# Two groups of stores move to ScalarE's DMA queue in a four-layer graph network

## The chip, the cores and the metric

The kernel runs on one core of a Trainium2 chip. The metric is device time in microseconds (us) from the start of the program to its end, as the median of several runs. Five engines work side by side, each through its own list of instructions in order: TensorE (PE in the profile), VectorE (DVE), ScalarE (ACT), GpSimd (POOL) and SyncE (SP). SP, ACT and POOL can also issue DMA transfers, each on a queue of its own.

## The reference

A graph of 2708 nodes with 512 features goes through four layers, each of the form `x = layernorm(x + layer(x, adj))`, all in fp32. Layer 0 is a graph attention autoencoder with four heads of 128 features, and the change lies in it. Cut to what matters:

```python
Xw = einsum('hnd,hde->hne', Xh, W)
f1 = einsum('hnd,hd->hn', Xw, V[:, 0, :, 0])
f2 = einsum('hnd,hd->hn', Xw, V[:, 1, :, 0])
sig = sigmoid(f1[:, :, None] + f2[:, None, :])
att = masked_softmax(adj * sig, adj != 0)      # both patterns are adj
Xa = einsum('hij,hjd->hid', att, Xw)           # first attention pass
# batchnorm, mlp block -> emb
Y = einsum('hij,hjd->hid', att, Yh)            # second pass, same att
# times W, elu, mlp block; then layers 1, 2 and 3
```

Layer 1 multiplies by the normalised adjacency matrix, layer 2 is attention over a masked score matrix, layer 3 is full attention with the adjacency as a bias.

## The kernel before, in words

The attention matrix of layer 0 is never whole. It is formed in blocks: a block has 128 of the nodes j on the partitions (22 blocks, the last with 20 rows) and one half of the nodes i along the free axis (1354 columns). Two heads, a "pair", are done together, so a block's tile `t` has 2 x 1354 columns. The loops of `attention_pass` run over the halves `hf`, then the pairs `p`, then the 22 blocks in the order of `ORDER`, in which the short block stands in the middle.

A block is formed in `form`: the adjacency block `a` is loaded by SP (L379); when the pair is the first one of the first pass (`prepare`), VectorE marks the zeros of `a` with large negative numbers (L395, L396) and POOL stores the result to `adj_d` in DRAM (L400), from where later passes load it. ScalarE computes a tanh for each head from the broadcast row `f1b` and the column `f2h` (L407), VectorE combines it with `a` (L415), and ScalarE takes the exp in place (L416). Then TensorE multiplies by the values (L503, twelve matmuls a block) and, in the first pass, sums with a column of ones (L540). The pool of `t` has four buffers and that of `a` four in the first pass.

The exponentials of the blocks in `KEPT` are stored to DRAM as `kept_...` in the first pass (L485) and loaded in the second (L488) in place of being formed again. Of the first pair, five places of 22 are kept in each half (4, 8, 11, 14, 18), so ten stores in all, one of them in each half of the short block. Of the second pair it is eight in each half. A full store is 1354 KB.

Before the passes, `project` loads the inputs on SP's queue: the transposed features in six chunks, the weights, the first two adjacency blocks and the parameters. `f1_rows` makes the rows of f1 for a chunk (L263, copied to `stage` by VectorE in L270). Those of the first half are stored to the DRAM tensor `f1_d` (L275), and two loads on SP (L277, the variable `spread`) broadcast them to all partitions as `f1b`, one for each head of the first pair. `values_of` makes the values `xw` and the columns `f2h`; ScalarE or VectorE copies them out of PSUM (L294, L298). The last blocks' values, and the rows of f1 of the second half, are made in `rest`, whose instructions on VectorE are put behind the first block's L415.

The order on each engine is set by a scheduler that works from the program's order and estimated times, bound here and there by `tc.issue_after`, which puts an instruction behind another one on the same engine. Waits between engines and for buffers are made from the tiles' use.

Of the kernel before, what the change touches and what calls it, by code (L numbers as in the profile page):

```python
# [29 lines left out]
def gnn_stack_kernel(  # L30
# [25 lines left out]
    nc = tc.nc  # L56
    N, F = x.shape
    H = w0.shape[1]
# [119 lines left out]
    with ExitStack() as l0:  # L178
# [8 lines left out]
        f1_d = dram.tile([H, N], F32, name="f1_d")  # L187
# [31 lines left out]
        def project(att, psum):  # L219
# [39 lines left out]
            def f1_rows(ci, dst):  # L259
                c0, w = CHUNKS[ci]  # L260
                pf = psum.tile([P, BANK], F32, tag=f"psm{ci % 2}", name="pf")
                for h in range(H):
                    nc.tensor.matmul(  # L263
                        pf[32 * h : 32 * h + 32, :w],
                        wv1[:, h, :],
                        xT_sb[:, h, c0 : c0 + w],
                        start=True,
                        stop=True,
                    )
                nc.vector.tensor_copy(dst[:, :w], pf[:, :w])  # L270

            h0, w = HSPAN[0]
            for ci, (q0, _) in enumerate(HCH[0]):
                f1_rows(ci, stage[:, q0:])
            nc.sync.dma_start(f1_d[:, h0 : h0 + w], stage[0 : 32 * H : 32, :w])  # L275
            for k in range(HP):
                spread = nc.sync.dma_start(  # L277
                    f1b[k][:, :w], f1_d[k, h0 : h0 + w].partition_broadcast(P)
# [63 lines left out]
        def attention_pass(values, first, att, psum, finish, f1b=None, blocks=(), spread=None, rest=None, taken={}):  # L342
# [5 lines left out]
            def count(hf, jt, att, a=None):  # L348

                h0, w = HSPAN[hf]  # L350
                j0, n = BLOCKS[jt]
                if a is None:
                    a = att.tile([P, HW], F32, tag="a", name="a", bufs=3)
                    nc.sync.dma_start(a[:n, :w], adj_d[j0 : j0 + n, h0 : h0 + w])
                z = att.tile([P, HW], U8, tag="z", name="z", bufs=1)
                nc.vector.tensor_scalar(
                    z[:n, :w],
                    a[:n, :w],
                    -0.5 * BIG,
                    None,  # L360
                    ALU.is_lt,
                    ALU.add,
                    accum_out=zeros[:n, jt, hf : hf + 1],
                )
# [62 lines left out]
            def sum_tiles():  # L427
                return [
                    psum.tile([P, BANK], F32, tag=f"psm{k}", name="psm", bufs=1) for k in range(HP)
                ]  # L430
# [5 lines left out]
            for hf, (h0, w) in enumerate(HSPAN):  # L436
                for p in range(H // HP):
                    prepare = first and p == 0
# [25 lines left out]
                    for place, jt in enumerate(ORDER):  # L464
                        n = BLOCKS[jt][1]
# [5 lines left out]
                        tv = t[:n, :, :w]  # L471
                        kept = kept_d.get((hf, p, jt))
                        if kept is None or first:
                            rows = n if n == P else HR
                            with ExitStack() as order:

                                for ins in taken.values() if place == 2 else ():
                                    order.enter_context(tc.issue_after(ins.ins))
                                step = form(hf, p, jt, att, prepare, f1b, t[:rows, :, :w])
                            if rest is not None:  # L480
                                rest(step)
                                rest = None
                                sums = sum_tiles()
                            if kept is not None:
                                nc.gpsimd.dma_start(kept[:n, :, :w], tv)  # L485
                        else:
                            for r in range(0, P if n == P else HB * Q, P if n == P else Q):
                                nc.sync.dma_start(t[r : r + n, :, :w], kept[:n, :, :w])  # L488
                            if p == 0 and jt in KEPT[1]:
                                count(hf, jt, att)  # L490
# [118 lines left out]
        with (  # L609
            tc.tile_pool(name="att_a", bufs=2) as att,  # L610
            tc.tile_pool(name="ps_a", bufs=1, space=PSUM) as psum,
        ):
            f1b, blocks, spread, rest = project(att, psum)
            mlp_w = []
            taken = {}
            ft = feat_tile("ft")

            def keep(hf, p, po, sums):
# [49 lines left out]
                for k in range(HP):  # L668
# [4 lines left out]
                    for r, (q0, qw) in enumerate(SCH[hf]):  # L673
# [12 lines left out]
                        nc.vector.bn_stats(stats[:, h, SQ * hf + r, :], dst)  # L686

            attention_pass(xw, True, att, psum, keep, f1b, blocks, spread, rest, taken)
            scale1, mean1 = batch_scale(stats, G_ENC, "bn1")
            shift1 = batch_shift(scale1, mean1, B_ENC, "bn1")  # L690
# [31 lines left out]
        with (  # L722
# [58 lines left out]
            for ci, (c0, w) in enumerate(CHUNKS):  # L781
# [24 lines left out]
                while turned < NT and sum(BLOCKS[turned]) <= c0 + w:  # L806
                    j0, n = BLOCKS[turned]
# [54 lines left out]
            def decode(hf, p, po, rb):  # L862
# [168 lines left out]
                )  # L1031

            attention_pass(emb, False, att, psum, decode)
        dsum = small.tile([P, NT], F32, tag="dsum", name="dsum")
        nc.vector.tensor_reduce(dsum, zeros, AX.X, ALU.add)
# [8 lines left out]
    with (  # L1044
# [13 lines left out]
        with tc.tile_pool(name="l1a", bufs=1) as pre:  # L1058
# [4 lines left out]
            for ci, (c0, w) in enumerate(PIECES):  # L1063
# [10 lines left out]
                while turned < NT and sum(BLOCKS[turned]) <= c0 + w:  # L1074
                    it = turned
                    i0, n = BLOCKS[it]
# [30 lines left out]
        for g in range(0, NT, G):  # L1107
            group = range(g, min(g + G, NT))
            c0 = g * P
            w = min(N, c0 + G * P) - c0  # L1110
# [9 lines left out]
            for jt, (j0, m) in enumerate(BLOCKS):  # L1120
                if later and jt % 4 == 3:
                    y, n = later.pop(0)
# [12 lines left out]
                for it in group:  # L1135
                    n = BLOCKS[it][1]
# [9 lines left out]
            for it in group:  # L1146
                n = BLOCKS[it][1]
# [51 lines left out]
    def softmax_layer(  # L1199
# [245 lines left out]
        def end(st):  # L1445
# [19 lines left out]
            for b, it in enumerate(GROUPS[gi]):  # L1465
# [46 lines left out]
                def project(b=b, it=it, n=n):  # L1512
# [9 lines left out]
                    finish(it, ps[:n], rs[:n, b : b + 1])()  # L1522

                later.append(project)

        states = {}
# [34 lines left out]
    with (  # L1561
# [3 lines left out]
        for gi, group in enumerate(GROUPS):  # L1565
            for y, n in last_rows if gi == 1 else ():
                layer_norm(y, y, n)
            c0, w = GSPAN[gi]
            xt = work.tile([P, C, GW], F32, tag="xt", name="xt_g")
            for b, it in enumerate(group):  # L1570
                n = BLOCKS[it][1]
# [8 lines left out]
            for b, it in enumerate(group):  # L1580
                n = BLOCKS[it][1]
# [260 lines left out]
```

## Time and profile before

| | us |
|---|---|
| median of 3 runs | 3232.25 |
| lowest and highest | 3231.26 and 3234.68 |
| the profiled execution | 3233.64 |
| its span, first to last instruction | 3231.8 |

| engine | busy us | share of the span |
|---|---|---|
| PE, matmul | 3196.0 | 99% |
| DVE | 1929.0 | 60% |
| ACT | 1318.2 | 41% |
| POOL | 136.1 | 4% |

The page gives the busy time of each engine, a chain of work that ended last, and groups of instructions by line. A timeline lists instructions in order: start, length, engine, line, operation, output and inputs; in square brackets stands the idle time of the engine before the instruction and what ended it. In a chain of waits each row has a start, a length and what took it. `SPq`, `ACTq` and `POOLq` stand for an engine's sequencer, which also issues DMAs. `f_d` is the profile's name for `f1_d`, and `f_rows` for `stage`. A table of windows gives busy times, the granted TensorE clock, the mean busy share of the 16 DMA engines and what they moved, by stretch.

### The profile page before, as it was taken

What the parts mean: (1) busy time and instruction counts of PE and PEld (TensorE: products, weight loads), DVE (VectorE), ACT (ScalarE), POOL (GpSimd) and SP (SyncE); (2) the same over time, 40 slices, a digit from 0 to 9 for tenths busy, and PEclk for the clock granted to TensorE, in tenths of its full rate; (3) what the DMA queues carried; (4) which work ended last, traced back from release to release, by engine and by line L of the source; (5) the groups of instructions that cost most, each with busy time, mean ns of one, the idle gap of its engine ahead of it and who ended that gap; (6) DMA issues with size and microseconds to landing.
All of it is one profiled execution on the core that took longest, in us unless ns stands there. A gap on an engine that the chain in (4) does not pass through costs nothing.

```text
span 3231.8 us, 30335 instructions
## 1 busy us (share of the span) xinstructions
PE 3196.0 (99%) x10874; PEld 1714.4 (53%) x10874; DVE 1929.0 (60%) x3160; ACT 1318.2 (41%) x1498; POOL 136.1 (4%) x220
## 2 busy tenths in 40 slices
PE   8999999999999999999999999999999999999999
PEld 5444444444444446875555555554555555555554
DVE  7888987876686685444154677776344342542533
ACT  6898896477767451001142434442011020120211
POOL 1100100000000000000010000000000000000000
PEclk9999999999999999999999999999999999999999
DMA  8867875156546314540054444553211111111100
GB/s 284 313 218 257 292 243 198 60 178 224 198 165 210 142 57 121 144 110 1 0 155 117 128 132 139 148 161 94 75 43 32 44 35 38 43 30 46 34 24 20
DMA packets 175701, 400.35 MB, mean 124 GB/s; under 512 B 21274, under 2 KB 116454, under 8 KB 169214
## 3 DMA queue, kind: packets, MB, share of 16 engines
q1 hardware_dynamic: 158622, 315.64, 32.1%
q0 software_dynamic: 16496, 80.70, 6.5%
q8 instruction: 85, 1.39, 0.2%
q10 hardware_dynamic: 432, 2.08, 0.2%
q14 instruction: 66, 0.54, 0.1%
HBM read 315.46 MB, written 81.30 MB: 123 GB/s over the span
## 4 chain that ended last, share of the span: by engine, by line
PE 85%; issue 8%; DVE 3%; ACT 2%; DMA 1%; POOL 1%; SPq 0%; POOLq 0%; DVEq 0%; ACTq 0%
PE po L1407 24%; PE ps_s L1286 18%; PE po L503 16%; PE ps_nb L1139 7%; PE ps_wide L1188 5%; PE ps_hid L128 2%; PE ps_sup L1584 2%; PE ps_o L1515 2%; PE ps_dec L914 2%; PE ps_mlp L789 1%; PE psm L540 1%; PE ps_s L1278 1%; ACT t L416 1%; PE tp L1178 1%; DVE t L415 1%
## 5 line engine op out<-in xcount | busy, mean ns | idle before, releaser
L415 DVE SCALAR_TENSOR_TENSOR t<-t,a 128x2708 f32<-128x2708 f32 (+1 forms) x150 | 444.3, 2976 | 150.2 <-ACT t L407 145.0
L407 ACT ACTIVATE t<-f1b,f2h 128x1354 f32<-128x1354 f32 (+1 forms) x300 | 411.2, 1412 | 50.0 <-PE po L503 31.7
L503 PE MATMUL po<-t,xw 128*128 128x452 f32 (+3 forms) x1056 | 407.6, 549 | 4.7 <-ACT t L416 4.7
L416 ACT ACTIVATE t<-t 128x2708 f32<-128x2708 f32 (+1 forms) x150 | 368.0, 2455 | 99.2 <-DVE t L415 99.1
L1286 PE MATMUL ps_s<-sup,hT 128*128 128x384 f32 (+1 forms) x1176 | 407.5, 490 | 0.0
L1407 PE MATMUL po<-sup,e 128*128 128x512 f32 x882 | 407.0, 595 | 0.0
L1407 PE MATMUL po<-e,xs 128*128 128x384 f32 (+1 forms) x1176 | 406.1, 489 | 0.0
L503 PE MATMUL po<-t,emb 128*128 128x452 f32 (+3 forms) x1056 | 395.5, 543 | 3.8 <-ACT t L416 3.8
L1718 DVE SCALAR_TENSOR_TENSOR e<-a_cols,ps_s 128x384 f32<-128x384 f32 (+1 forms) x154 | 85.6, 556 | 450.5 <-PE ps_s L1286 427.7
L1286 PEld LDWEIGHTS ps_s<-sup,hT 128*128 128x128 f32 x1176 | 221.8, 190 | 164.2 <-issue 14.2
L1407 PEld LDWEIGHTS po<-e,xs 128*128 128x128 f32 x1176 | 222.2, 190 | 160.2 <-issue 5.8
L503 PEld LDWEIGHTS po<-t,xw 128*128 128x128 f32 (+1 forms) x1056 | 188.7, 189 | 212.7 <-issue 196.1
L503 PEld LDWEIGHTS po<-t,emb 128*128 128x128 f32 (+1 forms) x1056 | 192.9, 189 | 199.3 <-issue 191.2
L1407 PEld LDWEIGHTS po<-sup,e 128*128 128x128 f32 x882 | 160.4, 190 | 159.3 <-issue 137.1
L1286 PE MATMUL ps_s<-hT 128*128 128x384 f32 (+5 forms) x672 | 211.0, 461 | 0.9 <-ACT sup L1591 0.7
L1385 ACT ACTIVATE e<-e 128x384 f32<-128x384 f32 (+1 forms) x308 | 151.6, 522 | 116.4 <-DVE e L1384 113.5
L1139 PE MATMUL ps_nb<-hid_hi,at 128*128 128x512 f32 x484 | 185.4, 390 | 0.4 <-DVE at L1131 0.4
L1633 ACT ACTIVATE a_cols<-a_cols,neg_big 128x384 f32<-128x384 f32 (+1 forms) x154 | 94.6, 616 | 223.5 <-DMA a_cols<-in_adjT_dram 195.7
L1139 PE MATMUL ps_nb<-hid_lo,at 128*128 128x512 f32 x462 | 179.9, 389 | 0.0
L1384 DVE TENSOR_TENSOR e<-e,nmax 128x384 f32<-128x384 f32 (+1 forms) x308 | 163.1, 552 | 23.3 <-ACT nmax L1377 23.3
L108 ACT ACTIVATE ln_rstd<-ln_rstd 128x1 f32<-128x1 f32 (+1 forms) x88 | 17.3, 202 | 389.1 <-DVE ln_rstd L107 388.3
L1286 PEld LDWEIGHTS ps_s<-hT 128*128 128x128 f32 x672 | 123.2, 190 | 89.3 <-issue 20.8
(253 smaller groups left out, 3327.1 us busy)
## 6 DMA issues: line engine op xcount, KB each, us to landing
a<-adj_d SPq DMA_DIRECT2D x108, 677.0 KB
a_cols<-in_adjT_dram SPq DMA_DIRECT2D x378, 192.0 KB
kept<-t POOLq DMA_DIRECT2D x22, 1354.0 KB, 6.5
t<-kept SPq DMA_DIRECT2D x22, 1354.0 KB
a<-in_adjT_dram SPq DMA_DIRECT2D x42, 677.0 KB
adj_d<-a POOLq DMA_DIRECT2D x42, 677.0 KB, 5.8
raw<-in_adjT_dram SPq DMA_DIRECT2D x105, 256.0 KB
a_cols<-in_adjT_dram SPq DMA_DIRECT2D x63, 202.0 KB
```

Of the source, the lines that this page charges most:

```text
L407: tanh = nc.scalar.activation(tv[:, k, :], f1b[k][:n, :w], AF.Tanh, bias=f2h[:n, jt, h : h + 1], scale=0.5,)
L415: step = nc.vector.scalar_tensor_tensor(tv, tv, GUARD, ab, ALU.add, ALU.mult)
L416: exp = nc.scalar.activation(tv, tv, AF.Exp, scale=0.5)
L503: nc.tensor.matmul(po[HB * k + q][:, :qw], values[r : r + n, jt, h * P : (h + 1) * P], t[r : r + n, k, q0 : q0 + qw], start=(place == 0), ...
L1139: nc.tensor.matmul(pos[it][:n], at, half[:, jt, :], start=(jt == 0 and k == 0), stop=(jt == NT - 1),)
L1188: nc.tensor.matmul(ps[:, :width], w(c, o), xt(c), start=(c == 0), stop=(c == C - 1),)
L1286: nc.tensor.matmul(ps[:, b * P : w], keys[:, c, j0 : j0 + P], st["q"][:, c, b * P :], start=(c == 0), stop=(c == C - 1),)
L1384: nc.vector.tensor_tensor(e, e, st["nmax"][:, :w], ALU.add)
L1385: nc.scalar.activation(e, e, AF.Exp)
L1407: nc.tensor.matmul(out, lhsT, rhs, start=(k == 0), stop=(k == NT - 1))
L1633: nc.scalar.activation(a, a, AF.Identity, bias=neg_big[: a.shape[0]], scale=1.0e30)
L1718: nc.vector.scalar_tensor_tensor(e, a, 2.0, ps, ALU.mult, ALU.add)
```

## The change

The store of f1's rows of the first half (L275) is issued from ScalarE and not from SyncE. The ten stores of the first pair's kept exponentials (L485 with `prepare` true) are issued from ScalarE and not from GpSimd; the sixteen of the second pair stay on GpSimd. Nothing else is edited: the same bytes go to the same places, and the loads of `f1b` stay on SP.

```diff
             h0, w = HSPAN[0]
             for ci, (q0, _) in enumerate(HCH[0]):
                 f1_rows(ci, stage[:, q0:])
-            nc.sync.dma_start(f1_d[:, h0 : h0 + w], stage[0 : 32 * H : 32, :w])
+
+            nc.scalar.dma_start(f1_d[:, h0 : h0 + w], stage[0 : 32 * H : 32, :w])
             for k in range(HP):
                 spread = nc.sync.dma_start(
                     f1b[k][:, :w], f1_d[k, h0 : h0 + w].partition_broadcast(P)
...
                             if kept is not None:
-                                nc.gpsimd.dma_start(kept[:n, :, :w], tv)
+
+                                queue = nc.scalar if prepare else nc.gpsimd
+                                queue.dma_start(kept[:n, :, :w], tv)
                         else:
```

## The prediction

> **What bounds the kernel now.** I read the page first: TensorE (PE) is busy in 3196.0 of 3231.8 us, so an edit moves the end only where it moves PE's work. Then I asked for PE's idle stretches in the first 560 us, where the moved stores lie (they are issued between 18.67 and 395.95 us). PE has a start in which it runs ahead of its data, and one hole that names a store of the kept exponentials. The chain of waits over the first 45 us shows the start:
>
> ```profile
> 17.99 0.02 issue
> 18.02 0.64 DVE f_rows L270
> 18.65 0.02 issue
> 18.67 5.93 DMA f_d<-f_rows
> 24.59 0.02 issue
> 24.61 0.34 SPq L277
> 24.95 0.06 issue
> 25.01 7.73 DMA f1b<-f_d
> 32.74 0.03 issue
> 32.77 1.43 ACT t L407
> 34.20 0.02 issue
> 34.23 2.98 DVE t L415
> ```
>
> Columns are start, length, what. The store of f1's first rows is only 21.2 KB, yet it takes 5.93 us. Until it has landed SP may not issue the two broadcast loads of f1b. Those take until 32.74, then come the tanh and the first scalar_tensor_tensor (L415). The `rest` work on VectorE is queued behind that L415, and PE's first attention matmul (L503) starts at 43.38.
>
> Why 5.93 us: the table of windows for 15 to 24 us has a DMA share of 1.00 at 377 GB/s. The packet records show SP's queue without a hole until about 24, and the store's own 5416 byte packets at 23.7 to 24.1, the last of the queue. The store waits behind inputs that SP queued earlier.
>
> The second place, timelines of PE, ACT and POOL around 315 to 329 us, in this order of lines:
>
> ```profile
> 315.24 0.53 POOL L400 DMA_DIRECT2D adj_d<-a  x1 [8.28 <-DVE a L396]
> 315.76 0.53 POOL L485 DMA_DIRECT2D kept<-t  x1
> ...
> 325.06 1.43 ACT L407 ACTIVATE t<-f1b,f2h 128x1354 f32<-128x1354 f32 x1 [3.00 <-DMA kept<-t]
> ...
> 328.88 4.82 PE L503 MATMUL po<-t,xw 128*128 128x452 f32 x12 [1.89 <-ACT t L416]
> ```
>
> The exp of that block ended at 314.34 (311.88 + 2.46). POOL first waited for VectorE's adjacency block and issued that store, then the kept one 1.42 us after its exp. The kept store landed 9.20 us later. A tanh that needs the buffer waited 3.00 us, and PE 1.89 us. Other PE holes of the first pass (0.93 at 236.40, 0.96 at 363.05, 0.93 at 486.44) name an exp behind the 20-row block, not a store.
>
> [...] two queues do alternate from 34 to 36.5 us, but POOL's store issued at 29.46 moved its first packet at 33.96, after 1539 KB of SP's loads. [...] from 38 to 43 us, after 2.94 us without a matmul, the granted clock is 0.50.
>
> **Part 1: f1's rows on ACT's queue (L275).** Removed from SP: one issue of 0.64 us, and SP's wait for VectorE's copy (3.3 us), which held nothing else, as the next SP items wait for this store anyway. Added to ACT: one issue. The nearest row is ACT's own f1b load (L453, three issues of 326 to 344 ns); the dearest is SP's 0.64. In that stretch ACT does the xw copies, 0.58 us each with 0.31 us of waiting for PE between them, so three copies absorb it; without that cover it is 0.64 us. If the issue stands one copy too early in ACT's order it waits for the rows (18.65), about 2 us after the copy that begins at 16.64. Queued behind it are ten more copies; PE waits for them, as pxw has three PSUM buffers. The copies end at 28.34 and the first tanh can't begin before that, so I take 0 and keep 1 us as the upper end.
>
> Landing: issue at 18.7, first packet 1.9 us later (ACT's f1b load of 151.92 began to move at 153.85)[...], 0.5 us to the release: about 22. Bounds: [...] 24.6 if the store still waits for all of the earlier inputs. Then SP issues the f1b loads (0.84 us for both)[...], and they follow the inputs without a gap at about 24.2, and ahead of the adj_d store issued at 23.89. 1354 KB at 365 KB per us (the 377 GB/s above) are 3.7 us: landed by about 28.5, against 32.74. If they share with that store (677 KB more), by 29.8.
>
> What is late next: ACT ends its copies at 28.34, two tanh of 1.42 end at 31.2. VectorE's row decides:
>
> ```profile
> 31.53 0.69 DVE L294 COPY xw<-pxw 128x512 f32<-128x512 f32 x1 [0.98 <-PE pxw L285]
> 32.14 0.15 DVE L298 TENSOR_SCALAR f2h<-pxw 128x4 f32<-128x4 f32 x1
> 34.23 2.98 DVE L415 SCALAR_TENSOR_TENSOR t<-t,a 128x2708 f32<-128x2708 f32 x1 [1.94 <-ACT t L407]
> ```
>
> If the order on VectorE stays, L415 begins behind that copy at 32.25 and not at 34.23: 2.0 us, all of its 1.94 us wait. With L415 ahead of the copy it would begin at 31.2: 3.0 us. After it VectorE and PE go hand in hand to 43.38, so PE starts its attention earlier by the same. From 44 to 170 PE is busy in 126.00 of 126.00 us, so the shift is kept. PE's idle stretch of 2.94 us shrinks by it too; if the half clock goes with it, the 5 us at 0.50 save up to 1 us more (2.5 of PE's own time, but VectorE sets most of that stretch). I take **-2.0**, bounds 0 and -4.0.
>
> **Part 2: ten kept stores on ACT's queue (L485).** Removed from POOL: ten issues of 0.53 us; POOL is idle 96% of the time, and its adj_d stores no longer have a kept store between them. Added to ACT: ten issues of 0.33, each behind the exp it stores. Where the trace doesn't show it is the wait: the issue has to wait until the exp's writes are done, so the next tanh, now overlapping the exp's end by about 0.1 us, can't be under way:[...] 0.55 us when the store stands directly behind its exp, 0 when it stands behind the next tanh. Queued behind it are the next tanh pair, then L415 on VectorE, then exp, then PE.
>
> What covers it: PE needs 6.03 us a block in these two stages, ACT 4.98 (2 x 1.41 + 2.45, less overlaps), and ACT waits for PE to free a buffer of t: 0.94 us a block at 68.02, 74.03, 80.07, 104.13 and 110.15, and after 341.14 too. In other blocks it waits for L415, 0.4 us each from 376 to 404. All ten stores have 3 or more blocks between them, each with 1.05 us to spare. So 10 x 0.55 = 5.5 us of ACT is hidden but for the stretch around 314 us where PE has no lead: **+0.3**. Bounds 0 and +5.5 by these prices. Below nothing is possible too, and is the next point.
>
> The hole at 328.88: on ACT the store is issued at about 314.8, 1 us earlier[...]. From 315.5, a load of 677 KB, the kept 1354 and the adj_d 677 are in flight: 2708 KB at 365 are 7.4 us, all landed by 323, the kept one not last, say 322. The tanh then starts at 322 and not 325.06, and its exp ends at 325.8, before PE is ready at 326.99. The 1.89 us hole closes: **-1.9**, bounds 0 and -1.9. PE is busy before and after, so it is kept; next late is the 0.96 at 363.05, which stays.
>
> **Sum.** -2.0 + 0.3 - 1.9 = -3.6 us. The profiled execution took 3233.64 (span 3231.8 and 1.8 around it): 3230.0. It is 1.4 above the median of the three runs, 3232.25, from which the forecast is 3228.65. A measurement of this kernel can tell about 0.2% from no change, 6.5 us.
>
> **The rivals.** (a) As summed: 3228.65. Chance 0.40.
> (b) The small store still waits for inputs[...], as POOL's store of 29.46 did. Part 1 is then worth nothing: -1.9 + 0.3, 3230.65. For it: that 1539 KB row. Against: 34 to 36.5. The move is made, and does not do what it is for. Chance 0.24.
> (c) All ends are good: L415 first (-3.0), the half clock gone (-1.0), the hole (-1.9), no ACT cost, and adj_d stores that land sooner by the 0.53 they now wait: -6.5 or a little more, 3225.5. Against: VectorE's order has to change. Chance 0.18.
> (d) Slower: ACT's queue blocks. If an issue takes not 0.33 but what SP's took[...] (2.49 at 9.03, 3.40 at 11.90), the tanh behind a kept store comes 3.6 us late. PE's lead over the exp is about 2.0 us in the first half (exp ends at 65.76, PE takes the block near 67.8), and 1.05 us a block comes back. It decides from some 2 us a store: then each store costs PE 1 to 1.6 us, ten of them 10 to 16, less the start's 2: +8, 3240.3. For it: DMA shares of 0.82 and 0.81 in these stages. Against: issues there take 0.32 on SP. Chance 0.18.
>
> **Numbers.** (a) and (b) are within 0.2%: 0.64. (c) makes faster 0.18, (d) slower 0.18. Both unknowns of part 1 and the wait of part 2 spread (a) and (b) from -6 to +3.5; the range takes in part of (c) and (d): 3223 to 3240.
>
> **What would show it.** L275's store should be on ACT's queue and land in 3 to 4 us; f1b's second load should land near 28.5 to 30; L415 start near 32.2; PE's first L503 near 41.4, and the half-clock stretch shorter. Around 315 us no tanh should wait for a kept store, and PE should have no hole near 327. Each prepared kept store should show ACT idle by 0.5 us or less. The forecast is wrong if PE gains new holes behind exp in 44 to 170 or 291 to 421, if the copies of xw wait for the rows' store, or if the order on VectorE around L415 differs.

## The result, and the profile after

| | before | after |
|---|---|---|
| median, us | 3233.47 (4 runs, 3231.26 to 3236.66) | 3247.43 (4 runs, 3245.59 to 3250.69) |
| profiled execution, us | 3233.64 | 3247.97 |
| its span, us | 3231.8 | 3246.2 |

The ratio is 1.0041, 95% interval 1.0029 to 1.0052: the change costs some 14 us. (The kernel before was run once more than for the prediction, hence its other median.) The forecast was 3228.65 in a range of 3223 to 3240, so it missed on the slow side. Lines of the kernel after stand one to three higher: L276 is the small store, L278 the loads of f1b, L401 the adj_d store, L408 the tanh, L416 the scalar_tensor_tensor, L417 the exp, L488 the kept store, L506 the attention matmul.

**The start did what the change says.** The chain of waits over the first 45 us of the kernel after (start, length, what):

```profile
18.47 4.76 DMA f_d<-f_rows
...
23.25 0.34 SPq L278
...
23.63 7.88 DMA f1b<-f_d
...
31.54 1.43 ACT t L408
...
32.99 2.98 DVE t L416
```

The small store takes 4.76 us and not 5.93, the f1b loads land at 31.51 and not at 32.74, and the first L416 starts at 32.99 and not at 34.23: 1.24 us sooner. PE's second attention block begins at 46.44, where before it began at 49.74.

**The hole near 329 us is gone.** The kernel after has no PE hole (idle time of TensorE ahead of a matmul) between 291 and 380 us, and no tanh there waits for a kept store; how much of that the queue explains is taken up below.

**And seven holes have come.** PE's timeline of the kernel after, windows 30 to 240, 240 to 480 and 480 to 545 us, rows with over 1.5 us idle before them in the square brackets (two of 0.47 and 0.56 at 401 and 465 are left out), and with 111.50 the matmuls behind the short block:

```profile
102.48 4.82 PE L506 MATMUL po<-t,xw 128*128 128x452 f32 x12 [1.60 <-ACT t L417]
111.50 6.51 PE L506 MATMUL po<-t,xw 128*128 128x452 f32 x12
139.28 4.82 PE L506 MATMUL po<-t,xw 128*128 128x452 f32 x12 [1.90 <-ACT t L417]
240.07 11.06 PE L506 MATMUL po<-t,xw 128*128 128x452 f32 x24 [2.45 <-ACT t L417]
380.70 6.51 PE L506 MATMUL po<-t,xw 128*128 128x452 f32 x12 [2.95 <-ACT t L417]
497.03 11.06 PE L506 MATMUL po<-t,xw 128*128 128x452 f32 x24 [2.87 <-ACT t L417]
```

Each hole waits for an exp. Look at the lengths too: twelve matmuls take 4.82 us, but 6.51 in two rows, and twenty-four take 11.06 where before they took 9.37 (486.44 us). That is 1.69 us each, four times: there the half clock is on, a granted clock of 0.50, for 3.41 us from 111.53, 241.24, 381.19 and 497.24. PE's waits for an exp from 44 to 541 us, first before and then after (total, times, longest):

```profile
PE po L503 <- ACT t L416: 4.7, 4, 1.9
```

```profile
PE po L506 <- ACT t L417: 12.8, 7, 3.0
```

The sum up to the first transpose of the next stage (tp_w, 541.31 before, 553.60 after, so 12.3 us late): 8.1 of holes, 4 x 1.69 = 6.8 of half clock, less 3.3 of the start, are 11.6; 0.7 isn't attributed. The other 2.1 of the span's 14.4 come later, where no store moved. There the granted clock is 0.50 for 6.83 us near 873 in after, and for 3.41 us near 1153 in before, which makes 1.7 of the 2.1.

**Why the exps are late** is seen on ScalarE around the first hole. The timelines of ACT, before and then after:

```profile
85.07 2.45 ACT L416 ACTIVATE t<-t 128x2708 f32<-128x2708 f32 x1
87.42 2.72 ACT L407 ACTIVATE t<-f1b,f2h 128x1354 f32<-128x1354 f32 x2
90.05 2.45 ACT L416 ACTIVATE t<-t 128x2708 f32<-128x2708 f32 x1
```

```profile
85.22 1.41 ACT L408 ACTIVATE t<-f1b,f2h 128x1354 f32<-128x1354 f32 x1
85.34 0.33 ACTq L488 DMA_DIRECT2D kept<-t  x1
89.72 2.46 ACT L417 ACTIVATE t<-t 128x2708 f32<-128x2708 f32 x1 [3.10 <-DVE t L416]
92.09 7.98 ACT L408 ACTIVATE t<-f1b,f2h 128x1354 f32<-128x1354 f32 x6
99.98 7.15 ACT L417 ACTIVATE t<-t 128x2708 f32<-128x2708 f32 x3
```

Before, two tanhs and an exp alternate. After, the kept store takes 0.33 us and lies beside the tanh that began 0.12 us earlier, so it costs nothing. But then ScalarE waits 3.10 us for VectorE, does six tanhs in a row, and only then three exps. The exp before the bunch ends at 92.18 and the next at about 102.4; PE uses one every 6.03 us, took the last at 94.78, and waits until 102.48. The compute instructions have another order, which no line of the diff asks for. The compiled list of ScalarE, from its start to the block of the first hole (T tanh, E exp, K kept store, a number is a repetition):

```
before  T4 E T2 E T2 E T3 E T2 E T2 E T2 E T2 E T E T2 E T2 E T2 E ...
after   T4 E T2 E T2 E T3 E T2 E T K E2 T5 E2 T K E T6 E3 K T5 E2 T K E T5 ...
```

From the first store on, tanhs and exps come in bunches. VectorE's list changes with it, two or three prepares (L396, L397) before two or three L416 in a row instead of one and one. Why the scheduler chose this order is not shown.

### The profile page after: what moved, and what is told of

Its sections match the earlier page's. It is cut to its first block, busy times and chain, and to the rows that moved or that the text cites. A ratio compares the mean times of both kernels' runs of the same rounds, so it can differ in the third digit from the quotient of the medians.

```text
span 3246.2 us, 30340 instructions
## 1 busy us (share of the span) xinstructions
PE 3201.6 (99%) x10874; PEld 1715.9 (53%) x10874; DVE 1926.5 (59%) x3160; ACT 1316.2 (41%) x1498; POOL 131.8 (4%) x210
## 4 chain that ended last, share of the span: by engine, by line
PE 80%; issue 13%; DVE 3%; ACT 2%; DMA 2%; POOL 1%; SPq 0%; POOLq 0%; DVEq 0%; ACTq 0%
PE po L1410 24%; PE ps_s L1289 18%; PE po L506 12%; PE ps_nb L1142 7%; PE ps_wide L1191 4%; PE ps_sup L1587 2%; PE ps_dec L917 2%; PE ps_o L1518 2%; PE ps_hid L128 2%; PE ps_mlp L792 1%; DVE t L416 1%; POOL adj_d L401 1%; PE ps_s L1281 1%; ACT t L417 1%; ACT t L408 1%
## 5 line engine op out<-in xcount | busy, mean ns | idle before, releaser
L416 DVE SCALAR_TENSOR_TENSOR t<-t,a 128x2708 f32<-128x2708 f32 (+1 forms) x150 | 443.1, 2972 | 146.0 <-ACT t L408 143.9
L506 PE MATMUL po<-t,xw 128*128 128x452 f32 (+3 forms) x1056 | 414.6, 557 | 13.6 <-ACT t L417 12.8
L408 ACT ACTIVATE t<-f1b,f2h 128x1354 f32<-128x1354 f32 (+1 forms) x300 | 409.4, 1412 | 42.0 <-PE po L506 33.1
L417 ACT ACTIVATE t<-t 128x2708 f32<-128x2708 f32 (+1 forms) x150 | 367.2, 2455 | 115.7 <-DVE t L416 115.4
L506 PE MATMUL po<-t,emb 128*128 128x452 f32 (+3 forms) x1056 | 398.4, 546 | 3.8 <-ACT t L417 3.8
L506 PEld LDWEIGHTS po<-t,xw 128*128 128x128 f32 (+1 forms) x1056 | 191.2, 192 | 225.5 <-issue 199.4
L506 PEld LDWEIGHTS po<-t,emb 128*128 128x128 f32 (+1 forms) x1056 | 194.3, 191 | 200.9 <-issue 193.0
```

The costliest lines, as they stand in the source:

```text
L408: tanh = nc.scalar.activation(tv[:, k, :], f1b[k][:n, :w], AF.Tanh, bias=f2h[:n, jt, h : h + 1], scale=0.5,)
L416: step = nc.vector.scalar_tensor_tensor(tv, tv, GUARD, ab, ALU.add, ALU.mult)
L417: exp = nc.scalar.activation(tv, tv, AF.Exp, scale=0.5)
L506: nc.tensor.matmul(po[HB * k + q][:, :qw], values[r : r + n, jt, h * P : (h + 1) * P], t[r : r + n, k, q0 : q0 + qw], start=(place == 0), ...
```

## The experiments

My theory, 'order': the loss is the new order of ScalarE's and VectorE's compute, which the scheduler chose once the stores stood in ScalarE's list. The rival, 'store': the stores themselves hold ScalarE up or collide with other transfers. Ratios are to the kernel before, each with its 95% interval; the medians of before in the four groups (e1 to e4, e5 to e7, e8 to e10, e11 and e12) were 3235.27, 3235.23, 3233.69 and 3233.37. A ratio need not be the quotient of two medians (0.9997 and 0.9994 in e1). Each trace is of one execution, which can lie some us from its kernel's median; where that matters it is said.

### One half of the change alone

```diff
 e1:
-            nc.sync.dma_start(f1_d[:, h0 : h0 + w], stage[0 : 32 * H : 32, :w])
+            nc.scalar.dma_start(f1_d[:, h0 : h0 + w], stage[0 : 32 * H : 32, :w])
 e2:
-                                nc.gpsimd.dma_start(kept[:n, :, :w], tv)
+                                queue = nc.scalar if prepare else nc.gpsimd
+                                queue.dma_start(kept[:n, :, :w], tv)
```

> Only the store of f1's rows is on ScalarE's queue. Both theories (order of the compute instructions; cost of the stores on ScalarE's queue) expect the start's gain alone: the rows' store lands in about 4.8 us, PE's second block of the first pass begins about 3 us sooner than 49.74, no half clock in the first 50 us, and the time is 2 to 3.5 us under the kernel before. If it is not faster, the gain at the start is lost later.

Measured: 3233.16, ratio 0.9997 [0.9989, 1.0005]. The second block begins at 46.23 us, 3.5 earlier than in the profile of before, but the hole near 329 grew to 2.71 (plus 0.30 ahead of it) and two half-clock stretches follow, at 328 and 362 (twelve matmuls take 6.51 and 7.77 us, for 4.82); 2.5 us behind before at tp_w. (This execution, of 3238.07, was the slowest of thirteen.) The expected 2 to 3.5 us are not shown: the ratio can't be told from 1.

> Only the ten kept stores are on ScalarE's queue. Both theories expect the whole loss here: 14 us of the change plus the 3 of the start, so 15 to 18 us over the kernel before, with PE holes behind exp near 102, 139, 240, 380 and 497 us.

Measured: 3252.51, ratio 1.0051 [1.0038, 1.0064], with ten holes behind exp between 100 and 510 us. The kept stores' half makes the whole loss. In the traces ScalarE's order of compute is exactly that of after in e2 and that of before in e1; VectorE's differs from it in two places.

### The order without the stores, the stores without the order

Tanhs, exps, prepares (L395, L396) and scalar_tensor_tensors of the first pass are collected in `made` and tied in a given order (T tanh, E exp, Z and A the two prepares, S the scalar_tensor_tensor); a NoSync edge fixes which is issued first.

```diff
+            for order in (ACT_ORDER, DVE_ORDER) if first else ():
+                seen, last = dict.fromkeys("TEZAS", 0), None
+                for kind, count in re.findall(r"([TEZAS])(\d*)", order):
+                    for _ in range(int(count or 1)):
+                        ins = made[kind][seen[kind]].ins
...
+                            tc.add_manual_dep(ins, last.name, mybir.DependencyInfo(
+                                mybir.DependencyClass.NoSync, mybir.DependencyReason.DATA), reason="order")
```

e4 is the kernel before, all stores where they were, with the two lists of after; e3 has the kept stores on ScalarE with the lists of before.

> All stores stay where they were before (GpSimd and SP), but the same edges bind the two engines' compute instructions of the first pass to the order that they have in the changed kernel. Theory order: 12 to 18 us over the kernel before, with the same PE holes. Theory stores: within 3 us of the kernel before.

Measured: 3252.08, ratio 1.0051 [1.0037, 1.0064]. PE's waits for exp from 44 to 541 us in e4 (total, times, longest; L522 and L432 are the same two lines):

```profile
PE po L522 <- ACT t L432: 18.1, 8, 3.3
```

No store was moved, and the loss is that of e2 to 0.5 us. Its holes stand where e2's stand: 103, 120, 141, 243, 384, 407, 473 and 505 us, against 103, 120, 142, 245, 387, 407, 472 and 503 in e2 (not all of them equally long), which has two more under 0.5 us. The order is enough to make the loss.

> The ten kept stores are on ScalarE's queue, and edges bind tanh and exp on ScalarE and the adjacency work and L415 on VectorE, in the first pass, to the order they had in the kernel before. Theory order: the loss is gone, the hole near 328 us closes, 0 to 3 us under the kernel before. Theory stores (the wait for the exp, the issue on ScalarE[...]): the loss stays, 12 us or more over it.

Measured: 3249.56, ratio 1.0044 [1.0031, 1.0056]: the expectation missed. In the two stretches where the ten stores lie it came true: no PE hole from 44 to 170 us, one of 1.08 from 291 to 421. But holes came at 172 to 244 and at 464 to 498 us, where the second pair is worked on. VectorE's timeline of e3 ahead of the hole at 200 shows why:

```profile
189.57 0.94 DVE L687 TENSOR_TENSOR ft<-ft,rb 128x340 f32<-128x340 f32 x2 [3.07 <-DMA rb<-rs_d]
190.42 0.92 DVE L689 BATCH_NORM_STATS2 stats_a<-ft 128x6 f32<-128x340 f32 x2
...
194.59 5.85 DVE L431 SCALAR_TENSOR_TENSOR t<-t,a 128x2708 f32<-128x2708 f32 x2
```

Twelve small instructions on the first pair's results, which I hadn't tied, were put ahead of L431; the first waits 3.07 us for a DMA, and everything behind it with it. The scheduler had moved what was left free, and e3 doesn't yet separate the two theories; that needs the whole order.

### The whole order tied, and another queue

All 1447 compute instructions of ScalarE and 3094 of VectorE are tied, by name, to the place that they have in the kernel before:

```diff
     with tile.TileContext(nc) as tc:
         gnn_stack_kernel(tc, *args)
+        keep_order(tc)   # NoSync edges along the two lists of the kernel before
```

e5 is e2 with this, e6 the whole change with this. e7 has no ties and puts the ten kept stores on SyncE's queue (`queue = nc.sync if prepare else nc.gpsimd`).

> The ten kept stores on ScalarE's queue as in the change, f1's rows left on SyncE; and every ScalarE and VectorE compute instruction of the whole program (1447 and 3094 of them) tied by order-only edges to the place that it has in the kernel before, so not tanh, exp, prepare and scalar_tensor_tensor alone as in the run that tied those. Theory 'order' (the loss is only the new order of compute instructions that the scheduler chose around the moved stores; the stores themselves cost ScalarE nothing): no PE hole over 1 us behind exp before 700 us other than those of before (236, 363, 486), the hole near 329 us (1.9 us) gone, so 0 to 3 us under the kernel before, ratio 0.999 to 1.000. Rival 'store' (a store in ScalarE's list holds ScalarE up or collides with other transfers, and tying all of the order can't help): again 10 to 18 us over, ratio 1.003 to 1.006.

Measured: 3234.76, ratio 1.0001 [0.9993, 1.0009]. Against e2, the same stores on the same queue, 0.50% is gone, and in the trace both engines' compute has exactly the order of before. The expected 0 to 3 us of gain are not shown, and one expectation missed: the hole near 329 is closed, but a new one of 1.75 at 350 us (a tanh waits for a later kept store) and a half-clock stretch at 361 (6.51 us for twelve matmuls) take it back.

> The whole change (f1's rows and the ten kept stores on ScalarE's queue), with all ScalarE and VectorE compute instructions tied to the order of the kernel before. Theory 'order': the two gains are kept, some 3.3 us at the start (place 1's attention matmuls begin that much earlier, no half clock near 38 us) and 1.9 us of the hole near 329 us, so 3 to 6 us under the kernel before, ratio 0.998 to 0.999, and the run is the fastest of all. Rival 'rhythm' (the start's lead is taken back by a later hole with half clock, as the rows store alone showed at 327 us): ratio 0.9995 to 1.001. Rival 'store': ratio over 1.003.

Measured: 3232.96, ratio 0.9991 [0.9983, 0.9999]: the only run whose interval lies on the fast side. The change as it was given has 1.0041. PE's timeline of e6, the short block and the row behind it, which has the half clock, then all rows up to 541 us with a hole, but for that of tp_w:

```profile
106.92 1.79 PE L657 MATMUL po<-t,xw 20*128 20x452 f32 x12
...
109.92 6.51 PE L657 MATMUL po<-t,xw 128*128 128x452 f32 x12
...
234.99 5.20 PE L657 MATMUL po<-t,xw 128*128 128x452 f32 x13 [0.92 <-ACT t L568]
...
350.47 4.82 PE L657 MATMUL po<-t,xw 128*128 128x452 f32 x12 [0.78 <-ACT t L568]
...
360.46 4.82 PE L657 MATMUL po<-t,xw 128*128 128x452 f32 x12 [0.90 <-ACT t L568]
...
483.85 9.36 PE L657 MATMUL po<-t,xw 128*128 128x452 f32 x24 [0.93 <-ACT t L568]
```

The account against before: 3.1 us early at the second block (46.64), 1.7 lost to the half clock at 110, so 1.4 early at 235 (234.99 for 236.40); the hole of 1.89 gone, one of 0.78 new; 2.6 early at tp_w (538.72). Both gains are there, and half of the first is lost again to a half clock, as 'rhythm' had it, though here without a hole; the ratio lies between what 'order' and 'rhythm' foretold.

> The ten kept stores of the prepare stages go out on SyncE's queue and not on GpSimd's; ScalarE's list holds none of them, and f1's rows stay where they were. The scheduler's order of ScalarE and VectorE compute then stays that of before but for about three places. Theory 'order': no general loss, within 3 us of the kernel before; each store may hold back the loads queued behind it on SyncE until its exp has ended, which the leads of 5 blocks should hide. Rival 'early store' (it is the store's earlier or hardware-run transfer that collides with the loads, from whichever queue): 10 us or more over the kernel before, as with ScalarE's queue.

Measured: 3234.78, ratio 1.0001 [0.9993, 1.0009]. The hole near 329 is gone here too, and tp_w is 2.4 us earlier in the profile, which the times can't tell from nothing. SyncE's queue is of the same kind as ScalarE's (the profile calls both hardware_dynamic, q1 and q10, and GpSimd's q0 software_dynamic), but SyncE's list holds no compute, and from there the stores cost nothing that can be measured. With e5 this rules out 'store' to within 0.1%, and 'order' stands.

### How many stores it takes

`queue` is nc.scalar for fewer of the ten: e8 for block 4 of the first half alone, e11 for blocks 4 and 8 of it, e12 for all five of the first half.

```diff
-                                queue = nc.scalar if prepare else nc.gpsimd
+                                queue = nc.scalar if prepare and hf == 0 and jt == 4 else nc.gpsimd      # e8
+                                queue = nc.scalar if prepare and hf == 0 and jt in (4, 8) else nc.gpsimd # e11
+                                queue = nc.scalar if prepare and hf == 0 else nc.gpsimd                  # e12
```

> Only one of the ten kept stores, that of the first prepared block (first half, block 4, issued near 63 us), goes out on ScalarE's queue; the other nine stay on GpSimd's, and f1's rows on SyncE's. The compiled order changes for the next 20 blocks or so: right behind the store come two exps, then five tanhs, then two exps, where the kernel before has two tanhs and one exp in turn. Theory 'order': the price isn't proportional to the number of stores; a single one already makes one or two PE holes of 1 to 3 us behind exp between 80 and 170 us, and one half-clock stretch, so 2 to 8 us over the kernel before (ratio 1.0005 to 1.0025). Rival 'store' (each moved store costs its own share): a tenth of the whole loss, 1 to 2 us, with a hole right behind the store.

Measured: 3234.07, ratio 1.0001 [0.9993, 1.0009]. The order is bunched (`E2 T5 E2 T4 E2`), and there is no hole over 1 us behind exp up to 235 us: my 'order' expectation of 2 to 8 us missed. (A half-clock stretch comes at 111, behind the short block and without a hole, as in e6.) ACT's timeline of e8:

```profile
74.10 6.67 ACT L407 ACTIVATE t<-f1b,f2h 128x1354 f32<-128x1354 f32 x5
80.67 2.44 ACT L416 ACTIVATE t<-t 128x2708 f32<-128x2708 f32 x1
```

The exp ends at 83.11; PE would have been ready for it at 83.04 (its sums began at 81.76 and take 1.28 here), and begins at 83.17. The first bunch uses the lead up to the last tenth.

> Two of the ten kept stores on ScalarE's queue, those of blocks 4 and 8 of the first half (issued near 63 and 85 us); the others on GpSimd's, f1's rows on SyncE's. ScalarE's compiled list is that of the whole change up to the bunch behind the second store: two tanhs, one exp with a store, six tanhs in a row, then three exps. Theory 'lead' (the first bunch uses up the lead that ScalarE's exps have over PE, the second, 22 us later, finds it used up): a PE hole of 1 to 2 us behind exp at 102 to 105 us, which the run with one store doesn't have, then no hole over 1 us until 235; 1 to 4 us over the run with one store at 234 us on PE's clock, ratio to before 1.0003 to 1.0012. Rival (each bunch is covered by itself, and only five or more add up): no hole at 102 to 105 us, ratio 0.9997 to 1.0003.

Measured: 3235.34, ratio 1.0005 [0.9997, 1.0013]. PE's timeline of e11:

```profile
86.61 4.82 PE L504 MATMUL po<-t,xw 128*128 128x452 f32 x12 [1.74 <-ACT t L416]
106.61 4.82 PE L504 MATMUL po<-t,xw 128*128 128x452 f32 x12 [1.84 <-ACT t L416]
```

The second bunch makes the foretold hole, at 106.6 since this execution ran later from its start. The first bunch made one as well, which it didn't in e8 and should not have by 'lead'; nor did it in after, e2 and e4, while in e12 it did, and why is not shown. At 239.02, behind the next short block, e11 is 3.7 us behind e8 (235.35): 1.8 of the start and 3.6 of the two holes, less 1.7 of e8's half clock. The times of the two don't differ by more than their intervals, so only the traces show the holes.

> The five kept stores of the first half on ScalarE's queue, the five of the second half on GpSimd's, f1's rows on SyncE's. Theory 'order': the holes of the run with all ten stores up to 290 us are there (near 103, 120, 141 and 245 us), with their half-clock stretches, and none of those behind 300 us but the two of before near 329 and 363; some 9 to 11 us over before at 290 us, of which 7 to 11 stay at the end, ratio 1.002 to 1.0035. Rival (the loss comes late, from the second half): under 3 us, ratio under 1.001.

Measured: 3243.88, ratio 1.0031 [1.0019, 1.0042]. Holes at 86, 106, 123, 143 and 246 us, two with half clock (143: 6.51 us for twelve matmuls, 246: 11.06 for twenty-four); behind 300 us only the 0.96 (with half clock here, 6.51 us at 373) and the 0.93 of before remain. The loss is what 'order' foretold. By the times alone a price of some 1.6 us for each store would fit too: one, two, five and ten stores have 0.01, 0.05, 0.31 and 0.51%, within the intervals of 0.05% a store. What speaks against a price of the store itself is that the ten cost nothing on ScalarE with the old order (e5), and that the traces show holes behind bunches and none in e8.

### A version with both gains?

The rows on ScalarE's queue and the kept stores on SyncE's, e9 without ties, e10 with the whole order tied:

```diff
-                                queue = nc.scalar if prepare else nc.gpsimd
+                                queue = nc.sync if prepare else nc.gpsimd
```

> f1's rows on ScalarE's queue as in the change, the ten kept stores on SyncE's queue and not on ScalarE's; nothing ties the order, and the scheduler's own is that of before but for three places of ScalarE and three of VectorE. Theory 'order': both gains and no loss: 3 us at the start and 1.9 us of the hole near 329 us, so 2 to 5 us under the kernel before, ratio 0.9985 to 0.9995. Rival 'rhythm' (the start's lead is taken back by a later half-clock stretch, as in both runs with the rows moved so far): ratio 0.9993 to 1.0005.

> As the run with f1's rows on ScalarE's queue and the kept stores on SyncE's, but with all ScalarE and VectorE compute instructions tied to the order of the kernel before. Theory 'order': the same to within 2 us as without the ties, since the two orders hardly differ; ratio 0.9983 to 0.9995. If the three places matter, it differs by more.

Measured: e9 3231.69, ratio 0.9996 [0.9988, 1.0005]; e10 3231.88, 0.9996 [0.9987, 1.0004]. Both are within the noise of before, so the expected gain of 1.5 to 5.5 us is not shown. The profile of e10, of the fastest of its thirteen executions, is 4.6 us early at tp_w (536.70), with 232.31 and 481.84 for the holes at 236.40 and 486.44; that of e9, the second slowest of its thirteen, is 0.3 us early, with half clock at 110 (6.51 us for twelve matmuls) and for 6.83 us at 359 (7.77). So the traces show the gains, and that the half clock can take them back; of e6, e9 and e10 no one is shown to be the best.

## Why the prediction was wrong, step by step

- **The step that failed is part 2's '+0.3'**, and in it the premise that the tanhs, L415 and exps keep their order. The prediction costed the moved store as something that stands in a fixed list: an issue of 0.33, at most 0.55 with its wait; the wait was my estimate, and no trace of before shows it. That price was too high if anything: the wait for the exp was said to keep the next tanh from being under way, but in after all ten stores are issued 0.03 us after their exp, eight of them 0.12 us into the next tanh, and ScalarE shows no gap for them. But a store in ScalarE's list changed the list. e4 shows that the new order by itself costs 0.51%, e5 that the stores without it cost nothing that can be measured. The bounds, 0 to +5.5, took in no such case. The term's measured size in after: 12.8 us of holes against 2.8 (4.7 without the 1.9 that has a term of its own), and 6.8 of half clock, so +16.8; 1.7 of it, the stretch at 111, may not belong here, since e6, e8 and e9 have it too without a hole.
- **The cover.** '1.05 us to spare in each block' is an average over blocks of an even rhythm. It isn't there for a bunch: six tanhs put 7.98 us between two exps, with three exps behind them in a row, while PE takes one block every 6.03 us.
- **Rival (d) had the sign and not the mechanism.** It gave 3240.3 for a ScalarE that blocks in long issues (those of SP in before are 2.49 us at 5.67, 2.22 at 9.03 and 3.40 at 11.90). The issues took 0.30 to 0.35 us in the prepare stages. Only the small store at 18.47 took 1.05, above the 0.64 that I gave as its dearest, and nothing waited for it.
- **What the prediction said would prove it wrong** named places: 'new holes behind exp in 44 to 170 or 291 to 421' came at 102, 139, 381 and 401. The two at 240 and 497, where the second pair is worked on, it did not look for. It named the order on VectorE around the first L415 alone; that one did stay. I asked whether one queue's order would change at one place, and never whether the program's would.
- **Part 1, -2.0.** The mechanism was right, its times too early: the store landed at 23.23 (foretold 22, of which about 0.9 was my estimate, shown by no trace; bound 24.6), f1b at 31.51 (28.5 to 29.8), L416 at 32.99 (32.25). The mis-sized term is the f1b loads: 7.88 us, much as before (7.73), and not the 3.7 to 5 that I worked out from bytes over bandwidth. In after the DMA engines were fully busy then, but moved far less than the 377 GB/s that I took (the last two columns are the busy share and GB/s):

```profile
25.00:27.00 2.00, 2.00 (x21) 2.00 (x20) 0.81 (x3) 1.38 (x3) 0.00 (x0) 1.00 1.02 227
27.00:29.00 2.00, 2.00 (x20) 2.00 (x19) 2.00 (x5) 1.12 (x3) 0.00 (x0) 1.00 0.95 282
```

  The store's own landing was off by its delay and not by a queue ahead of it, so rival (b) did not come true: in after its eight packets begin to move between 22.39 and 22.76 us, while SP's queue moves too (174 KB from 22.0 to 22.5 us, 175 in the next half). In the five profiles with the store on ScalarE its issue starts between 18.00 and 19.25, its first packet follows 3.92 to 3.96 us later, and SP's next issue 4.77 to 4.82 later, each time. In the nine with it on SyncE its issue starts between 17.79 and 19.36, and its first packet moves at 23.1 to 23.5 whenever that was, as behind a queue. I had taken 1.9 for the delay, from a quieter stretch (1.7 by the profile's own zero; the packet times in the prediction lie 0.24 too late). Why it is 3.9 here is not shown; 1.05 of it is the issue. PE gained 3.3, more than the 1.24, since no half clock fell there (granted clock from 36 to 44 us 1.00, in before 0.58). That isn't the store's doing alone: with the rows unmoved the second block began at 46.9 to 47.3 in four profiles without that half clock (e2, e4, e5, e8: 1.00) and at 47.7 to 49.7 in five with it (before 0.58; e3, e7, e11, e12 0.79); with the rows moved, at 45.5 to 46.6 in five profiles, none with it. The store itself is worth about 0.9 us at an equal clock, 1.8 on the average of all nine; the 1.7 between the two groups of nine is what one half-clock stretch costs.
- **The hole at 328.88, -1.9.** It is gone in after, e5, e6, e7, e9 and e10, and in e6 the tanh that began at 325.06 begins at 321.48 (foretold 322). But the reason given, a store that lands sooner on its own queue, isn't shown: in e6 that store is issued at 311.43, 0.03 us after its exp, and the tanh still waits 2.79 us for it. With the stores on GpSimd's queue the wait was 3.00, 3.72, 2.73, 1.69 and 1.36 us (before, e1, e11, e8, e12), and in e8 and e12 there was no PE hole either. And what is late next was not the 0.96 at 363: in e5 and e6 a tanh near 345 us waits 2.5 to 2.8 us for the next kept store, which gives back up to 1.75.
- **The half clock.** What sets it off is not shown, and a hole's length alone does not. In the traces every stretch from 44 to 542 us lasts 3.41 or 6.83 us, and in before and after they begin whole multiples of 3.413 us apart (38, 41 and 34 of them between the four of after, 327 between those at 37.26 and 1153.42 us in before). Of the 18 holes of 2.24 to 4.30 us that the fourteen profiles have there, 17 have a stretch with them; that of 2.33 in e3 has none, and holes of up to 1.90 us have none, but for those behind a short block. At the start, holes of 2.78 to 3.09 us in e2, e4, e5 and e8 have none (granted clock 1.00), that of 2.94 in before has one. In after three of the four stretches follow holes of 2.45 to 2.95 us; that at 111.50 and e6's at 109.92 have no hole over 0.1 us in the 7 us ahead of them, but the short block. I had counted the half clock at the start only as a part of the start, with 5 us where the trace has 6.83; where it follows a hole of after it adds 1.69 us, more than half of the hole itself.

## What to carry to other kernels

Where a scheduler orders the program, an instruction that is moved to another engine's list can reorder that list's compute: before costing the instruction itself, compare the compiled order of every engine it leaves, joins or feeds, and if it changed, cost the new order. Here the ten stores could be issued at no measurable cost from an engine whose list holds no critical compute (SyncE, e7), and from ScalarE only with the good order tied, and all of it: in e3 what was left free was moved. A lead that hides one bunch may be used up by the next, so that a reordering hidden in one place need not be hidden in ten.

## What was not expected of the hardware

- An issue on ScalarE's sequencer ran beside ScalarE's own activation: 0.33 us, begun 0.12 us into a tanh (85.34 in after), without a gap in ScalarE's work.
- TensorE's clock also fell to half without an idle hole, behind the short block with 20 rows on the partitions (109.92 in e6: 6.51 us for twelve matmuls, 4.82 at full clock; granted clock 0.50 from 111 to 113 us). In before the block behind it, at 113.01, has full clock. Of the 28 short blocks of the first pair in the fourteen profiles, 12 have the half clock behind them. What decides is not shown; an estimate from the traces of before and after goes with it in their four cases. The matmuls and sums of 20 rows last 3.06 us. Continue the grid of 3.413 us, on which the stretches of an execution begin, to its short blocks, and take the step of the grid with the least time in matmuls of more rows: that time is 14% of the step at 108.50 in after, with the half clock behind it, and 34, 29 and 53% at 110.02 and 359.02 in before and at 362.63 in after, with full clock. Four cases give no limit, and the ends of matmuls are modelled. So whether a short block costs 1.7 us differs from execution to execution, and it is one of the things that took back the gains of e1 and e9.
- The start differs by up to 2.9 us between executions of code that is the same up to there (46.87 to 49.74 us for the second block). A gain of a few us at the start is read from several profiles, or not at all.
